# Heads of a two-layer graph network: PSUM banks in a fixed round, and conv1's constants moved ahead of the first statistics

## The chip, the cores and the metric

The kernel runs on one core of one Trainium2 chip. The metric is the device time of one execution, in microseconds. A profile is one execution recorded by the hardware profiler; its span is the time between its first and last recorded instruction, and the execution's own time is a little longer.

The engines are named as the profile names them: PE is TensorE's matmuls, PEld its weight loads, DVE is VectorE, ACT is ScalarE, POOL is GpSimd, SP is SyncE, which here only issues transfers. Lines such as L227 are lines of the kernel before the change.

## The reference

Two layers work on `x` of 128 graphs x 128 nodes x 256 channels, with an adjacency matrix per graph. Only the first steps of layer 0 matter here:

```python
h = jnp.maximum(_layernorm(x, axis=-1), 0.0)
# layer 0, on h
xc = jnp.transpose(h, (0, 2, 1))
c = relu(bn1(conv1d(xc, conv1_w, pad=0)))          # 1x1
c = bn2(conv1d(c, conv2_w, pad=8))                 # 17 taps
x_conv = transpose(relu(c + xc))
# message passing on h (distances, exp, mask, matmul), then a GRU gate
x = x + gru(concat([x_conv, x_nmp]), h)
# layer 1: graph convolutions on five groups of the first 25 nodes
```

`bn(h) = h * scale + shift` with `scale = g / sqrt(v + eps)` and `shift = b - m * scale`, per channel.

## The kernel before, in words

The graphs are worked in 32 blocks of four (`NBLK` = 32, `BB` = 4). The 17-tap convolution is done as products of spectra: 68 frequencies over a length of 136. The kernel has these stages:

1. The heads, to about 277 us. For each block: load, layer norm, transpose, conv1 with bn1 and relu, and the transform of the result into spectra. Between these steps the taps of conv2 are transformed into spectra as well, in 16 pieces of four groups each, 64 groups in all, and written to DRAM (`vd`).
2. The spectral products (`spectral`), to about 454 us, which read `vd` back as `v` and write `yd`.
3. The gates of the 32 blocks with messages, edges and layer 1 woven in, to the end.

In the heads the order on every engine is the order in which the code is written (`tc.manual_schedule()`). Behind them only GpSimd's order is by hand for a while, and the rest is ordered by Tile's scheduler. The scheduler may also place instructions of later code among the heads: it does so with the short chain on the fusion weights (L472 to L486).

The steps that the prediction names are these.

- `bank()` (L89) takes one tile of a PSUM pool with eight buffers, each a whole bank of 128 x 512 floats. A tile waits until the buffer that it gets has been read by the engine that empties it. Which of the eight buffers a tile gets is left to Tile.
- `weight_spectra` (L157) makes one piece of the taps' spectra: four groups of eight matmuls (L164) into four banks. ScalarE copies three of the banks out (L172) and VectorE the fourth (L170), except in a piece's last group, where ScalarE copies all four. When a piece is finished ScalarE issues the write of 2176 KB to `vd` (L174). `some_spectra()` (L378) runs one group per call.
- `head_stats` takes the layer norm's mean and variance of a block on VectorE (L191, L192, L195) and the power -0.5 on GpSimd (L197). `head_norm` applies them on VectorE (L203). `head_turn` transposes the block into two banks (L213), and ScalarE reads them with a relu (L214).
- `head_conv1` multiplies half a block with conv1's weights `wc1` into one bank (L227). VectorE empties it, adding bn1's shift (L230). `head_relu` follows on ScalarE (L234).
- `head_spectra` transforms a block into four banks (L243). ScalarE and VectorE empty two banks each (L253, L251).
- `heads` (L256) loops over the blocks. Iteration i runs conv1 of half of block i, a group of tap spectra, conv1 of the other half, the turn of block i + 1, a second group, and `head_spectra` of block i - 1. Statistics run three blocks ahead, normalising two. Every eighth iteration has an extra group.
- `constants` (L115) is a generator with two steps. The first, on VectorE and GpSimd, works out scale and shift of both batch norms from `vec` (L122 to L127) and spreads bn1's over a tile `bnb` (L130). The second turns `bnb` with an identity into rows on TensorE (L134), which ScalarE copies to `bnr` (L135); VectorE multiplies `wc1` by the scale (L136) and adds two gate biases (L137).

Transfers into SBUF are issued by SP, in the order taps, x, `wc1`, `fd`, further x and taps, `fw`; `gt` and `vec` are issued by ScalarE's queue at the start.

The code around the start of the heads is this:

Of the kernel before, what the change touches and what calls it, by code (L numbers as in the profile page):

```python
# [8 lines left out]
F32 = mybir.dt.float32  # L9
# [4 lines left out]
P = 128  # L14
# [53 lines left out]
V_BN1, V_BN2, V_IH, V_HH, V_B1, V_B2 = 0, 8, 16, 22, 28, 48  # L68
# [6 lines left out]
def gnn_kernel(ctx: ExitStack, tc: tile.TileContext, io, out0: bass.AP, out1: bass.AP):  # L75
# [8 lines left out]
    front = ExitStack()  # L84
    hc = front.enter_context(tc.tile_pool(name="hc", bufs=1))
    dram = ctx.enter_context(tc.tile_pool(name="dram", bufs=1, space=bass.MemoryType.DRAM))
    psum = ctx.enter_context(tc.tile_pool(name="psum", bufs=8, space=bass.MemoryType.PSUM))

    def bank():  # L89
        return psum.tile([P, 512], F32, tag="bank", name="bank")  # L90

    def row(name, n):

# [17 lines left out]
    def constant_loads():  # L111
        nc.sync.dma_start(wc1, io["wc1"].rearrange("(c p) o -> p c o", p=P))
        nc.sync.dma_start(fd, io["fd"])

    def constants():  # L115


        for j, v0 in enumerate((V_BN1, V_BN2)):
            g, b, m, v = (vec[:, v0 + 2 * q:v0 + 2 * q + 2] for q in range(4))
            sc, sh = bn[:, j, 0, :], bn[:, j, 1, :]  # L120
            ve = cst.tile([P, C], F32, name=f"bnve{j}")
            nc.vector.tensor_scalar(ve, v, EPS, None, op0=ALU.add)  # L122
            rs = cst.tile([P, C], F32, name=f"bnrs{j}")
            nc.gpsimd.tensor_tensor(rs, ve, mhalf[:, :C], op=ALU.pow)
            nc.vector.tensor_mul(sc, g, rs)
            nc.vector.tensor_mul(ve, m, sc)
            nc.vector.tensor_sub(sh, b, ve)  # L127

        bnb = hc.tile([P, 2 * C, P], F32, name="bnb")
        nc.vector.tensor_copy(bnb, bn[:, 0].rearrange("p q c -> p (q c)")[:, :, None].to_broadcast([P, 2 * C, P]))  # L130
        yield
        psb = bank()
        for q in range(2 * C):
            nc.tensor.matmul(psb[:, q * P:(q + 1) * P], bnb[:, q, :], ident, start=True, stop=True)  # L134
        nc.scalar.copy(bnr.rearrange("p q d -> p (q d)"), psb)  # L135
        nc.vector.tensor_mul(wc1, wc1, bnr[:, 0:1, :].to_broadcast([P, C, D]))  # L136
        nc.vector.tensor_add(brz, vec[:, V_IH:V_IH + 4], vec[:, V_HH:V_HH + 4])  # L137
        yield

# [9 lines left out]
    def taps_load(pool, c, q, queue, split=1, amid=None):  # L149
        w2 = pool.tile([P, WCH // 4, P], F32, tag="w2", name="w2", bufs=3)  # L150
        for t in range(0, WCH // 4, WCH // 4 // split):
            queue.dma_start(w2[:, t:t + WCH // 4 // split], io["w2t"][:, c, q, t:t + WCH // 4 // split])
            if amid:
                amid.pop()()
        return w2
# [23 lines left out]
    def head_load(pool, ahead, i, queue):  # L179
        xs[i] = pool.tile([P, BB, D], F32, tag="ln", name="ln", bufs=ahead)  # L180
        queue.dma_start(xs[i], x[i])

    def head_stats(wk, i, parts=(0, 1)):

        for h in parts:
            if not h:
                stats[i] = (wk.tile([P, BB, 2], F32, tag="mv", name="mv", bufs=3),
                            wk.tile([P, BB, 6], F32, tag="st", name="st", bufs=2))
            mv, st = stats[i]
            for b in range(h * BB // 2, (h + 1) * BB // 2):  # L190
                nc.vector.bn_stats(st[:, b, :], xs[i][:, b, :])  # L191
                nc.vector.bn_aggr(mv[:, b, :], st[:, b, :])  # L192
            if h:
                ve = wk.tile([P, BB], F32, tag="ve", name="ve", bufs=2)
                nc.vector.tensor_scalar(ve, mv[:, :, 1], EPS, None, op0=ALU.add)  # L195
                rs = wk.tile([P, BB], F32, tag="rs", name="rs", bufs=3)
                nc.gpsimd.tensor_tensor(rs, ve, mhalf, op=ALU.pow)  # L197
                stats[i] = mv, rs

    def head_norm(i):  # L200
        mv, rs = stats.pop(i)
        for b in range(BB):
            nc.vector.tensor_scalar(xs[i][:, b, :], xs[i][:, b, :], mv[:, b, 0:1], rs[:, b:b + 1],  # L203
                                    op0=ALU.subtract, op1=ALU.mult)
# [149 lines left out]
    with front as es:  # L354
        hk = es.enter_context(tc.tile_pool(name="hk", bufs=1))
        xp = es.enter_context(tc.tile_pool(name="xp", bufs=1))
        X1 = xp.tile([P, C, NP_ - NB, 2, P], F32)
        order = es.enter_context(ExitStack())
        order.enter_context(tc.manual_schedule(engines={nc.gpsimd.engine}))
        early = es.enter_context(ExitStack())  # L360
        xe = early.enter_context(tc.tile_pool(name="xe", bufs=1, side="right"))
        X0 = xe.tile([P, C, NB, 2, P], F32)
        X = X0, X1
        with ExitStack() as ws:

            ws.enter_context(tc.manual_schedule())

            xk = ws.enter_context(tc.tile_pool(name="xk", bufs=1, side="right"))
            wp = ws.enter_context(tc.tile_pool(name="wp", bufs=1))
            ahead = 4  # L370
            todo = [(c, q) for c in range(C) for q in range(D // WCH)]
            nc.scalar.dma_start(gt, io["gt"])
            nc.scalar.dma_start(vec, io["vec"])

            taps = [taps_load(wp, *todo[0], nc.sync, split=4, amid=[lambda: head_load(xk, ahead, 0, nc.sync)])]
            spectra = []

            def some_spectra(k=1):  # L378
                for _ in range(k):
                    if not spectra and todo:  # L380
                        spectra.append(weight_spectra(wp, *todo.pop(0), taps.pop(0)))
                    if spectra and next(spectra[0], STOP) is STOP:
                        spectra.pop(0)
                        if len(todo) > 2:
                            taps.append(taps_load(wp, *todo[2], nc.sync))
                        some_spectra()

            constant_loads()
            head_load(xk, ahead, 1, nc.sync)
            taps.append(taps_load(wp, *todo[1], nc.sync))  # L390
            for k in range(2, ahead):
                head_load(xk, ahead, k, nc.sync)
            nc.sync.dma_start(fw, row("fw", 5))
            taps.append(taps_load(wp, *todo[2], nc.sync))
            head_stats(hk, 0)
            some_spectra()
            head_norm(0)
            consts = constants()
            next(consts)
            some_spectra()  # L400
            some_spectra()
            head_turn(hk, 0)
            head_stats(hk, 1)
            some_spectra()
            next(consts)
            head_norm(1)
            head_stats(hk, 2)
            some_spectra()
            heads(hk, xk, ahead, X, some_spectra)
            while spectra or todo:  # L410
                some_spectra()

        bp = es.enter_context(tc.tile_pool(name="bp", bufs=1, reuse_waits="tile"))
        spectral(bp, (X0, 0), 0, NB, {})
        early.close()
        gw = ctx.enter_context(tc.tile_pool(name="gw", bufs=1, side="right", reuse_waits="tile"))
        idm = gw.tile([P, N], F32)
        wms = gw.tile([P, C, 2, MW], F32)
        bms = gw.tile([P, 2, MW], F32)
        swm = gw.tile([P, 3, MW], F32)  # L420
        wih = gw.tile([P, 2 * C, 3 * D], F32)
        whh = gw.tile([P, C, 3 * D], F32)
        sw = [gw.tile([P, 3, 3, P], F32, name=f"sw{k}") for k in range(3)]

        def gate_loads():
            nc.sync.dma_start(wms, io["wms"].rearrange("(c p) (q o) -> p c q o", p=P, q=2))
            yield
            nc.sync.dma_start(idm, io["idm"])
            nc.sync.dma_start(bms.rearrange("p q o -> p (q o)"), row("bms", 2 * MW))
            for name, w in (("whh", whh), ("wih", wih)):  # L430
                for c in range(w.shape[1]):
                    yield
                    nc.sync.dma_start(w[:, c], io[name][c * P:(c + 1) * P])

        loads, sums = gate_loads(), gate_weights()

        def gate_steps(p):
            next(loads, None)
            if p in (36, 40, 44, 52, 56, 60, 64):
                next(sums, None)  # L440

        amid = {p: lambda p=p: gate_steps(p) for p in range(NB, NP_, 4)}
        spectral(bp, (X1, NB), NB, NP_, amid)
        for _ in sums:
            pass
        order.close()
# [773 lines left out]
```

## Time and profile before

| | us |
|---|---|
| three runs | 1884.16, 1883.59, 1886.41 (median 1884.16) |
| profiled execution | 1882.45 |
| its span | 1880.5 |
| PE busy | 1858.3 (99%) |
| PEld busy | 1593.0 (85%) |
| DVE busy | 1353.7 (72%) |
| ACT busy | 743.4 (40%) |
| POOL busy | 665.3 (35%) |

Busy times are shares of the whole span, over stages that have different limits. The ends of matmuls are modelled, so that a busy PE may hold a short stall; the distance between equal instructions of two iterations tells such a stall more surely. The row "PEclk" gives the TensorE clock that was granted, as a share of full speed.

In a timeline a row is: start us, duration us, engine, line, operation, output <- input, shape, count, and in brackets the idle time before it and what ended that.

### The profile page before, as it was taken

Reading aid. Unit: us, or ns where it says so; the run is one execution under the profiler, and the core shown is the slowest. Engines: PE = TensorE matmul, PEld = TensorE weight load, DVE = VectorE, ACT = ScalarE, POOL = GpSimd, SP = SyncE. Lnnn points to the kernel's source line nnn. Section 1 sums busy time; section 2 is a strip of 40 time slices with the busy share of each in tenths; the row PEclk is TensorE's granted clock in tenths of the full one; section 3 lists DMA queues with packets and bytes.
Section 4 is the critical chain, followed back from the end, with each engine's and each line's share of the span. In section 5 each row is a group of like instructions: output and inputs, shape, how many; then the busy total and the mean of one; then the engine's idle time right before and its main releaser. Section 6 shows DMA issues by size and latency. Waiting matters only on the chain.

```text
span 1880.5 us, 31012 instructions
## 1 busy us (share of the span) xinstructions
PE 1858.3 (99%) x10854; PEld 1593.0 (85%) x10854; DVE 1353.7 (72%) x3248; ACT 743.4 (40%) x1667; POOL 665.3 (35%) x803
## 2 busy tenths in 40 slices
PE   8999999999999999999999999999999999999998
PEld 6888888888888888888788888888788888888887
DVE  7787765455878888888656778787666678788643
ACT  4665651111443334333334433433343343334334
POOL 1111125676343544454212345444312344544200
PEclk9999999999999999999999999999999999999999
DMA  8878788997532233224234322333233333222125
GB/s 295 292 309 309 283 291 280 349 314 248 165 90 73 72 83 94 76 72 121 64 103 113 122 74 72 90 79 112 61 102 94 121 94 86 72 72 67 41 88 157
DMA packets 218330, 267.95 MB, mean 142 GB/s; under 512 B 105186, under 2 KB 181815, under 8 KB 216127
## 3 DMA queue, kind: packets, MB, share of 16 engines
q1 hardware_dynamic: 206079, 195.60, 36.1%
q10 hardware_dynamic: 12096, 70.36, 9.1%
q8 instruction: 87, 1.43, 0.3%
q14 instruction: 68, 0.56, 0.1%
HBM read 169.24 MB, written 96.67 MB: 141 GB/s over the span
## 4 chain that ended last, share of the span: by engine, by line
PE 93%; DVE 2%; DMA 2%; POOL 1%; issue 0%; SPq 0%; ACT 0%; DVEq 0%; POOLq 0%; ACTq 0%
PE bank L636 44%; PE bank L318 6%; PE bank L227 5%; PE bank L964 5%; PE bank L904 5%; PE bank L522 5%; PE bank L502 3%; PE bank L243 3%; PE bank L313 3%; PE bank L587 3%; PE bank L164 2%; PE bank L499 2%; PE bank L213 1%; PE bank L883 1%; PE bank L813 1%; PE bank L572 1%
## 5 line engine op out<-in xcount | busy, mean ns | idle before, releaser
L636 PE MATMUL bank<-t,sw 128*128 128x256 f32 x1152 | 290.9, 379 | 0.0
L649 POOL TENSOR_TENSOR u<-u,m 128x256 f32<-128x256 f32 x128 | 93.4, 730 | 499.2 <-ACT m L647 424.6
L636 PEld LDWEIGHTS bank<-t,sw 128*128 128x128 f32 x1152 | 210.6, 190 | 26.6 <-issue 2.3
L636 PE MATMUL bank<-t,wih 128*128 128x256 f32 x768 | 197.2, 379 | 0.0
L636 PEld LDWEIGHTS bank<-t,wih 128*128 128x128 f32 x768 | 143.4, 190 | 19.3 <-issue 0.5
L227 PE MATMUL bank<-wc,ht 128*128 128x256 f32 x512 | 125.5, 390 | 0.3 <-DVE wc L136 0.3
L310 POOL TENSOR_TENSOR vs<-v 128x256 f32<-128x256 f32 x134 | 98.1, 756 | 72.4 <-PE bank L313 38.1
L545 ACT ACTIVATE msg<-msg 128x512 f32<-128x512 f32 x64 | 36.9, 622 | 205.5 <-DVE msg L541 205.5
L636 PE MATMUL bank<-xc,wih 128*128 128x256 f32 x384 | 114.5, 380 | 0.0
L636 PE MATMUL bank<-t,whh 128*128 128x256 f32 x384 | 114.5, 380 | 0.0
L636 PE MATMUL bank<-xn,wih 128*128 128x256 f32 x384 | 114.2, 379 | 0.0
L964 PE MATMUL bank<-w,hh 128*125 128x256 f32 (+9 forms) x480 | 113.3, 379 | 0.0
L197 POOL TENSOR_TENSOR rs<-ve,mhalf 128x4 f32<-128x4 f32 x32 | 32.6, 1020 | 223.0 <-DVE ve L195 223.0
L636 PE MATMUL bank<-ht,whh 128*128 128x256 f32 x384 | 109.9, 380 | 0.0
L904 PE MATMUL bank<-ax,w 128*128 128x500 f32 (+8 forms) x416 | 107.0, 396 | 0.9 <-DMA w<-in_w_dram 0.9
L227 PEld LDWEIGHTS bank<-wc,ht 128*128 128x128 f32 x512 | 93.6, 192 | 15.3 <-DVE wc L136 0.6
L964 PEld LDWEIGHTS bank<-w,hh 128*125 128x125 f32 (+9 forms) x480 | 84.3, 177 | 18.0 <-issue 0.9
L682 ACT ACTIVATE nn<-nn,vec 128x512 f32<-128x512 f32 x64 | 46.2, 722 | 134.1 <-DVE nn L681 134.1
L307 DVE SCALAR_TENSOR_TENSOR s<-X 128x256 f32<-128x256 f32 x67 | 46.2, 691 | 66.5 <-PE bank L318 66.5
L654 DVE TENSOR_TENSOR u<-bank,u 128x256 f32<-128x256 f32 x128 | 53.5, 418 | 54.5 <-PE bank L636 54.2
L172 ACT COPY sp<-bank 128x272 f32<-128x272 f32 x208 | 66.7, 401 | 63.0 <-PE bank L164 61.9
L502 PEld LDWEIGHTS bank<-idm,ym 128*128 128x128 f32 x512 | 66.0, 196 | 26.4 <-issue 24.0
(206 smaller groups left out, 4449.0 us busy)
## 6 DMA issues: line engine op xcount, KB each, us to landing
vd<-sp ACTq DMA_DIRECT2D x16, 2176.0 KB
v<-vd SPq DMA_DIRECT2D x34, 1024.0 KB
w<-in_w_dram SPq DMA_DIRECT2D x40, 512.0 KB
ln<-in_x_dram SPq DMA_DIRECT2D x32, 512.0 KB
htd<-ht ACTq DMA_DIRECT2D x32, 512.0 KB
yd<-ys ACTq DMA_DIRECT2D x32, 512.0 KB
ht<-htd SPq DMA_DIRECT2D x32, 512.0 KB
ym<-yd SPq DMA_DIRECT2D x32, 512.0 KB
```

Source lines behind the costliest of these rows:

```text
L172: nc.scalar.copy(dst, s)
L227: nc.tensor.matmul(pv[:, bb, :], ht[:, c, b * N:(b + 1) * N], wc1[:, c, :], start=c == 0, stop=c == C - 1)
L243: nc.tensor.matmul(ps[:, bb * LW:(bb + 1) * LW], h1[:, 2 * h + bb, c * P:(c + 1) * P], fd, start=True, stop=True)
L310: nc.gpsimd.tensor_tensor(vs[:, c], vr[c], vi[c], op=ALU.add)
L313: nc.tensor.matmul(p1[:, :D], a[:, c], vs[:, c], start=c == 0, stop=c == C - 1)
L318: nc.tensor.matmul(ps[:, k * D:(k + 1) * D], u[:, c], w[c], start=c == 0, stop=c == C - 1)
L502: nc.tensor.matmul(ps[:, b * N:(b + 1) * N], ym[:, b, o * P:(o + 1) * P], idm, start=False, stop=b == BB - 1)
L522: nc.tensor.matmul(ps[:, b, :], d[:, b * N:(b + 1) * N], w, start=True, stop=True)
L636: nc.tensor.matmul(ps, w, d, start=n == 0, stop=n == len(pairs) - 1)
L649: nc.gpsimd.tensor_tensor(got["u4"], got["u2"], got["m5"], op=ALU.add)
L904: nc.tensor.matmul(pv[:, q - q0, :], w1s[k5 + g][:, c, q * P:(q + 1) * P], xv[:, c], start=c == 0, stop=c == C - 1)
L964: nc.tensor.matmul(ps[:n1, :D], hh[:, q, at:at + n1], w2s[k5 + g][:, q, :], start=q == 0, stop=q == HID // P - 1)
```

## The change

Three things are changed.

- While the heads run, `bank()` takes the banks from eight tags with one buffer each, in a strict round: tile n goes to bank n mod 8. When the heads are done this pool is closed, and a pool of eight buffers is opened as before, with waits kept per tile (`reuse_waits="tile"`).
- `constants` has three steps instead of two. The first works out bn1 alone and `bnb`; the second makes `bnr` and multiplies `wc1`; the third works out bn2 and the gate biases.
- The calls move. The first step comes ahead of the first block's statistics, the second behind the first group of tap spectra and ahead of the first normalising, the third behind the third block's statistics. One call of `some_spectra()` ahead of `heads` is dropped, so that four are left; the group that it ran is run later, by the loop.

```diff
-    psum = ctx.enter_context(tc.tile_pool(name="psum", bufs=8, space=bass.MemoryType.PSUM))
+    turns = ExitStack()
+    banks = [turns.enter_context(tc.tile_pool(name="turns", bufs=1, space=bass.MemoryType.PSUM)), 0]
 
     def bank():
-        return psum.tile([P, 512], F32, tag="bank", name="bank")
+        pool, n = banks
+        if n is None:
+            return pool.tile([P, 512], F32, tag="bank", name="bank")
+        banks[1] = (n + 1) % 8
+        return pool.tile([P, 512], F32, tag=f"bank{n}", name="bank")
...
     def constants():
-        for j, v0 in enumerate((V_BN1, V_BN2)):
+        def scales(j, v0):
...
+        scales(0, V_BN1)
         bnb = hc.tile([P, 2 * C, P], F32, name="bnb")
...
         nc.vector.tensor_mul(wc1, wc1, bnr[:, 0:1, :].to_broadcast([P, C, D]))
+        yield
+        scales(1, V_BN2)
         nc.vector.tensor_add(brz, vec[:, V_IH:V_IH + 4], vec[:, V_HH:V_HH + 4])
         yield
...
             taps.append(taps_load(wp, *todo[2], nc.sync))
+            consts = constants()
+            next(consts)
             head_stats(hk, 0)
             some_spectra()
+            next(consts)
             head_norm(0)
-            consts = constants()
-            next(consts)
             some_spectra()
             some_spectra()
             head_turn(hk, 0)
             head_stats(hk, 1)
             some_spectra()
-            next(consts)
             head_norm(1)
             head_stats(hk, 2)
-            some_spectra()
+            next(consts)
             heads(hk, xk, ahead, X, some_spectra)
...
+        turns.close()
+        banks[:] = [ctx.enter_context(tc.tile_pool(name="psum", bufs=8, space=bass.MemoryType.PSUM, reuse_waits="tile")), None]
```

## The prediction

> **What bounds the kernel now.** I read the page first (busy shares, then the chain that ended last), then the chain in order of time for the first 600 us, then timelines of single iterations, the waits of the DMA queue, and windows for the clock.
>
> ```profile
> PE 1858.3 (99%) x10854; PEld 1593.0 (85%) x10854; DVE 1353.7 (72%) x3248; ACT 743.4 (40%) x1667; POOL 665.3 (35%) x803
> PE 93%; DVE 2%; DMA 2%; POOL 1%; issue 0%; SPq 0%; ACT 0%; DVEq 0%; POOLq 0%; ACTq 0%
> ```
>
> TensorE carries 93% of the chain, so only its stalls can be won. Its idle time is 22.2 us of 1880.5, but a stalled matmul can also read as busy, so I measure stalls by the period of a loop. In the heads (33 to 277 us) the chain shows each iteration's `head_spectra` (L243):
>
> ```profile
> 41.68 2.05 PE bank L243 x16
> ...
> 49.60 2.06 PE bank L243 x16
> ...
> 58.44 2.05 PE bank L243 x16
> ...
> 83.13 2.06 PE bank L243 x16
> ...
> 92.69 2.05 PE bank L243 x16
> ...
> 100.62 2.05 PE bank L243 x16
> ```
>
> Periods: 7.92, 8.84, then 9.56 (an iteration with an extra group of weight spectra) and 7.93. From 92.69 to 148.18 seven iterations in a row take 7.93, with DVE 45.17 and ACT 34.76 busy of 55.49 us and not one wait of PE itself; so 7.93 is TensorE's own work. The timelines of a long and a short iteration show the rest:
>
> ```profile
> 53.31 0.50 PE L164 MATMUL bank<-gt,w 17*128 17x136 f32 x4
> 53.49 0.69 DVE L230 TENSOR_TENSOR h<-bank,bnr 128x512 f32<-128x512 f32 x1
> 54.23 0.73 PE L164 MATMUL bank<-gt,w 17*128 17x136 f32 x12 [0.42 <-DVE h L230]
> 62.15 0.74 PE L164 MATMUL bank<-gt,w 17*128 17x136 f32 x16
> ```
>
> At 53.31 the group starts, then needs the bank of the conv1 that ran just ahead of it, and waits until VectorE has emptied that bank (ends 54.18). At 62.15 the same group runs through.
>
> **The change, part by part.**
>
> *Strict round.* An iteration takes 16 banks: conv1, 4, conv1, 2 of `head_turn`, 4, 4 of `head_spectra`: two whole rounds. Each tile then waits for the one eight back. Going through an iteration that starts with `head_spectra` at 0 (rows from 108.47 on): conv1 starts at 1.9 and needs the first ScalarE copy of the second group, done by 1.4; the first group, at 3.8, needs copies done by 2.4; the second, at 7.2, needs L230 from 4.6 and copies from 5.5; `head_spectra` at 7.9 needs L230 from 7.2 for its second bank. Everything is free in time, the first with 0.4 to 0.5 us to spare. Removed: seven iterations of 8.84 (ending at 41.68, 58.44, 75.21, 166.57, 183.34, 200.10 and 216.87) at 0.91 each, 6.4 us; and two of 9.56, at 92.69 and 157.74, against 8.80 for the third of that kind (225.67), 1.5 us. Sum 7.9. After an extra group the four ScalarE copies of the group before it may end 0.1 to 0.2 late; I take 0.3 off for all.
>
> *One group later.* `some_spectra()` is called four times ahead of `heads` instead of five. The 64 groups stay; one of them, 0.87 us in an iteration ((7.93 − 6.18)/2, 6.18 being the period without groups, 255.82 to 262.01), moves behind the first `head_spectra`.
>
> *conv1's constants first.* Nothing is added or removed here, but every engine's order moves:
>
> ```profile
> SPq L152 <- DMA vec<-in_vec_dram: 0.9, 1, 0.9
> ```
>
> ```profile
> 10.60 0.16 DVE L122 TENSOR_SCALAR bnve<-vec 128x2 f32<-128x2 f32 x1
> 10.84 0.70 POOL L124 TENSOR_TENSOR bnrs<-bnve,mhalf 128x2 f32<-128x2 f32 x1 [1.58 <-DVE bnve L122]
> ```
>
> `vec` lands at 5.4 (SP's issue, held back 0.9 us by it, goes out at 5.42). From L122 to the end of the copy L130 is 1.85 us, so VectorE begins the statistics at 7.3, not 5.64, and all behind them on VectorE waits. TensorE ended its first group at 4.8 and now stands at L134 until 7.4 (before it stood until 5.98 for taps). Then, at the slow rates of the first 22 us: L134 2.0 to 9.4, two groups 2.5 to 11.9, turn 2.2 to 14.1, a group to 15.4, conv1 to 19.1. Before, that conv1 ended at 21.3: TensorE is 2.2 ahead.
>
> VectorE is not. Statistics 2.4 to 9.8, copy 0.4, `wc1` product 0.7, normalising 1.4 to 12.3 (before 10.7). In the built order the six fusion-weight instructions (L472 to L486) come next, with ScalarE's L476 between: 1.5; two copies 0.8: 14.7. Statistics 2.4, GpSimd's L197 1.2, normalising 1.4: 19.7. Statistics 2.4: 22.1. Then `scales(1)`: its power on GpSimd queues behind the statistics' own L197 (1.03 + 0.7), so VectorE stands 1.8 and reaches the first L230 at 24.8. Before:
>
> ```profile
> 22.43 0.68 DVE L230 TENSOR_TENSOR h<-bank,bnr 128x512 f32<-128x512 f32 x1
> ```
>
> In the strict round the sixth group takes that bank, so TensorE, there at 22.9 (warm) or 24.1, stands until 25.5. Conv1, group, conv1, turn, group follow with two waits of 0.5 for ScalarE's turn and for L230; the first `head_spectra` runs as if from 33.2, against 32.8, with one group less done. Loss 0.4 + 0.87 = 1.3. The rows of `fw` (landed somewhere before 20.08) leave 0 to 0.8 more if it lands after 12.7; I take 0, since 3.6 MB issued ahead of it at the window's 290 to 400 GB/s are through at about 12.
>
> *Behind the heads.* The built order of all engines is the same as before, and nearly all waits; the pool is opened again with per-tile waits. The last `vd` write goes out after the second relu of iteration 28, not after the last copies of 27: old time 257.4 instead of 251.71. With 6 us gained it starts at the same absolute time, its load of `v` lands by 268.3 as before, and TensorE asks at 271: cost 0, and up to 6 if that cover is gone. The rest is paced by TensorE and moves along.
>
> Sum: 7.9 − 0.3 − 1.3 = 6.3; I take 6.0, as each of the three start-up waits costs TensorE some 0.1 to refill.
>
> **A rule against it.** The clock rows:
>
> ```profile
> 460.00:461.00 1.00, 0.00 (x0) 0.00 (x0) 1.00 (x4) 0.97 (x2) 1.00 (x2) 1.00 0.12 31
> 462.00:463.00 1.00, 1.00 (x3) 0.24 (x2) 0.38 (x1) 0.00 (x0) 0.35 (x1) 0.50 0.92 313
> 467.00:468.00 1.00, 1.00 (x6) 0.35 (x9) 0.40 (x2) 1.00 (x2) 0.18 (x1) 0.50 0.89 337
> ```
>
> An idle of 1.74 us (to 461.06) was followed by a granted clock of 0.50 for some 6.7 us. The new wait of 1.4 to 2.6 us at 22.9 to 25.5 could do the same; 6.7 at half speed is 3.3 us, and the sum falls to 2.7. The Trainium skill, "TensorE: Matmul & The Clock Gate", section "HAM oscillation — how this bites in real kernels", asks only that gaps stay under about 3.4 us; by it the sum stays 6.0. The same page's "A second HAM failure mode: psum-queue depth-cycling" says that cycling through PSUM banks made the clock oscillate; here the granted clock is 1.00 over 32.84 to 249.45, gaps of 0.42 included, so no row supports it. I keep the loss for a rival, because in the sum the gap is short when the clock is still slow at 20 us.
>
> **Rivals.**
>
> 1. *The start-up gap slows the clock.* For: the row above. Against: from 20 to 25 us the slow clock fills the gap with work. 1884.2 − 2.7 = 1881.5.
> 2. *Slower: ScalarE holds conv1.* The strict round ties conv1's first bank to the first copy after ScalarE's relu in every iteration. For: only 0.45 us of room (copy done 101.90, weight load 102.39). Against: ScalarE is 63% busy and on time in every short iteration. It decides once ScalarE is over 0.45 late; at 0.85 late it costs 0.4 × 28 = 11 us: 1889.
> 3. *The loads of `v` swallow it.* For: DMA is 0.96 busy from 249 to 277. Against: 3 us of room. It decides when the first loads land 3 us later; at 6 the time is 1884.
> 4. *The banks were not the cause*, or the round moves the waits on to L230: the stalls stay and the start costs 1.3: 1885.5. Against: the one-to-one row 53.31 to 54.23.
>
> **How the numbers follow.** The profiled execution took 1882.45 us (span 1880.5 and 1.95 around it); less 6.0 it is 1876.45. The median of the three runs is 1884.16, 1.7 above it; less 6.0 it is 1878.2, my forecast. About 0.2%, or 3.8 us, is what a measurement can tell from no change: faster is below 1880.4, slower above 1887.9. Chances: forecast 0.60 (its own range 1875.5 to 1880.4), rival 1 0.17, rival 2 0.09, rival 3 0.07, rival 4 0.07. Faster: 0.60 and 0.05 of rival 1, whose loss may be partial. Same: 0.12 of rival 1, 0.07 of rival 3, 0.01 of rival 4. Slower: 0.09 and 0.06, what rivals 2 and 4 leave with other mishaps. The range goes from 1875.0 (no start-up loss, and the runs' own scatter) to 1884.5, which takes in rivals 1 and 3.
>
> **What would show it.** Right: every iteration of the heads at 7.93, the three with an extra group at 8.8 to 9.0, no "DVE h L230" in front of L164 after 40 us, the first L302 near 271, later stages as long as before. In the start: L134 at 7.4, the first conv1 at 15.4, the first L230 near 24.8, TensorE idle before it. Wrong: periods over 8 with ScalarE's copy as releaser (rival 2), clock 0.50 at 25 to 32 (rival 1), a wait on `v` at 271 (rival 3), or 8.84 still there (rival 4).

## The result, and the profile after

| kernel | median us | runs, lowest to highest | ratio to before, 95% interval |
|---|---|---|---|
| before | 1887.26 | 1883.59 to 1889.03 | |
| after | 1886.04 | 1880.52 to 1893.52 | 1.0001 [0.9989, 1.0013] |

The forecast was 6.0 us less; the runs show no difference within about 2 us. 1886.04 lies above the range of 1875.0 to 1884.5. The median of before itself came out 3.1 us above the one that the range was worked out from (1884.16); it is the ratio that tells, and by it nothing was gained. The profiled execution took 1891.3 us (span 1889.4), among the longest of its kernel; a second profile stands below ("After, again"). Line numbers of the kernel after are 5 to 10 higher: L134 became L140, L164 became L172, L227 L235, L230 L238, L243 L251, L174 L182.

The page of the kernel after, first the busy shares, then the shares of the chain by engine:

```profile
PE 1860.9 (98%) x10854; PEld 1595.3 (84%) x10854; DVE 1353.5 (72%) x3248; ACT 744.2 (39%) x1667; POOL 665.6 (35%) x803
...
PE 91%; DMA 3%; DVE 2%; POOL 1%; SPq 1%; issue 1%; ACT 0%; ACTq 0%; DVEq 0%; POOLq 0%
```

PE is still the bound, but has 2% less of the chain. Where the stalls of before were, the chain in order of time (start us, duration us, what) now has this:

```profile
37.58 2.05 PE bank L251 x16
...
45.51 2.05 PE bank L251 x16
...
53.44 2.05 PE bank L251 x16
...
125.93 2.05 PE bank L251 x16
...
146.14 2.05 PE bank L251 x16
...
163.71 2.05 PE bank L251 x16
```

Three things are to be seen. The periods are 7.93, and no iteration of 8.84 is left in the whole stage. The first `head_spectra` starts 4.7 us later than before (37.58 against 32.84). And two iterations took 20.21 between 125.93 and 146.14 instead of 15.86, and the two behind them, with an extra group, 17.57 instead of 16.73. The timelines show both losses. First the start, on TensorE, VectorE and GpSimd:

```profile
22.05 1.04 PE L221 MATMUL bank<-ident,ln 128*128 128x128 f32 x8
...
23.02 1.01 POOL L205 TENSOR_TENSOR rs<-ve,mhalf 128x4 f32<-128x4 f32 x1 [3.83 <-DVE bnve L127]
24.00 0.70 POOL L129 TENSOR_TENSOR bnrs<-bnve,mhalf 128x2 f32<-128x2 f32 x1
...
24.73 0.16 DVE L130 TENSOR_TENSOR bn<-vec,bnrs 128x2 f32<-128x2 f32 x1 [1.72 <-POOL bnrs L129]
...
25.27 0.69 DVE L238 TENSOR_TENSOR h<-bank,bnr 128x512 f32<-128x512 f32 x1
...
26.01 1.29 PE L172 MATMUL bank<-gt,w 17*128 17x136 f32 x16 [2.93 <-DVE h L238]
```

TensorE is done with the turn at 23.1 and stands until VectorE has emptied conv1's first bank. VectorE in turn waits 1.72 for GpSimd's power of the third step, queued behind that of the statistics, as the prediction had it. Windows of the same trace (us from:to, length, busy of PE, PEld, DVE, ACT, POOL, granted clock, DMA share, GB/s) show what follows:

```profile
24.00:25.00 1.00, 0.00 (x0) 0.00 (x0) 0.24 (x2) 0.00 (x0) 0.69 (x2) 1.00 1.09 470
...
26.00:27.00 1.00, 0.99 (x16) 0.97 (x16) 0.97 (x4) 1.00 (x2) 0.00 (x0) 0.50 0.86 341
...
34.00:36.00 2.00, 2.00 (x7) 1.50 (x6) 0.02 (x1) 0.00 (x0) 0.00 (x0) 0.50 0.00 0
36.00:37.00 1.00, 1.00 (x12) 0.83 (x14) 1.00 (x3) 0.49 (x1) 0.00 (x0) 1.00 0.00 0
```

The clock is 0.50 from 26 to 36 us. The second loss, on ScalarE and TensorE:

```profile
133.90 0.33 ACTq L223 DMA_DIRECT2D htd<-ht  x1
...
134.29 3.48 ACTq L182 DMA_DIRECT2D vd<-sp  x1
...
137.88 0.97 ACT L180 COPY sp<-bank 128x272 f32<-128x272 f32 x3 [2.97 <-issue]
...
138.31 3.68 PE L235 MATMUL bank<-wc,ht 128*128 128x256 f32 x8 [2.41 <-ACT sp L180]
```

The issue of a `vd` write, 0.33 us as a rule, occupied ScalarE's queue for 3.48 us. The copies behind it came late, and conv1 waited for the bank that the first of them frees. Behind this gap the clock fell again, to 0.60 and 0.55 in windows over 138 to 142 us, and conv1 took 3.68 instead of 1.99.

So this execution adds up, against the first profile of before: the start +4.7; the stage from the first `head_spectra` to the first spectral matmul 243.7 instead of 244.2, in which the round's gain is spent on the rows above and on a group more; and +4.7 behind the heads (1608.2 instead of 1603.5). Together +8.9, the difference of the spans.

### The profile page after: what moved, and what is told of

It is laid out like the page before. It is cut to its first block, busy times and chain, and to the rows that moved or that the text cites. A ratio compares the mean times of both kernels' runs of the same rounds, so it can differ in the third digit from the quotient of the medians.

```text
span 1889.4 us, 31044 instructions
## 1 busy us (share of the span) xinstructions
PE 1860.9 (98%) x10854; PEld 1595.3 (84%) x10854; DVE 1353.5 (72%) x3248; ACT 744.2 (39%) x1667; POOL 665.6 (35%) x803
## 4 chain that ended last, share of the span: by engine, by line
PE 91%; DMA 3%; DVE 2%; POOL 1%; SPq 1%; issue 1%; ACT 0%; ACTq 0%; DVEq 0%; POOLq 0%
PE bank L646 43%; PE bank L235 6%; PE bank L974 5%; PE bank L326 5%; PE bank L914 5%; PE bank L532 5%; PE bank L251 3%; PE bank L512 3%; PE bank L597 3%; PE bank L321 3%; PE bank L172 2%; PE bank L509 2%; PE bank L893 1%; PE bank L221 1%; PE bank L823 1%; PE bank L582 1%
## 5 line engine op out<-in xcount | busy, mean ns | idle before, releaser
L235 PE MATMUL bank<-wc,ht 128*128 128x256 f32 x512 | 130.6, 401 | 2.4 <-ACT sp L180 2.4
L235 PEld LDWEIGHTS bank<-wc,ht 128*128 128x128 f32 x512 | 96.6, 198 | 19.0 <-ACT sp L180 2.6
```

The costliest lines, as they stand in the source:

```text
L235: nc.tensor.matmul(pv[:, bb, :], ht[:, c, b * N:(b + 1) * N], wc1[:, c, :], start=c == 0, stop=c == C - 1)
```

## The experiments

Theory: the round takes out its 7.9 us, and three things give it back, namely the gap at the start with the clock's fall, the slow `vd` issues that the round ties to conv1, and later stages. Rivals: the round itself gains nothing; or the losses are chance events of one profile. Every profile is cut at two points, the first `head_spectra` ("start") and the first spectral matmul ("heads" up to it, "rest" behind it). Times in us, "heads" and "rest" as differences of points rounded to 0.1:

| kernel | start | heads | rest | span | ratio of the runs |
|---|---|---|---|---|---|
| before | 32.8 | 244.2 | 1603.5 | 1880.5 | |
| before, again | 32.7 | 244.3 | 1605.0 | 1882.0 | 0.9993 [0.9985, 1.0002] |
| after | 37.5 | 243.7 | 1608.2 | 1889.4 | 1.0001 [0.9989, 1.0013] |
| after, again | 35.7 | 239.1 | 1609.7 | 1884.5 | 0.9993 [0.9978, 1.0007] |
| round only | 32.7 | 240.9 | 1610.0 | 1883.6 | 0.998 [0.997, 0.9989] |
| constants only | 36.7 | 243.7 | 1607.4 | 1887.8 | 1.0028 [1.0016, 1.0041] |
| after, fifth group back | 33.4 | 238.8 | 1607.4 | 1879.6 | 0.9983 [0.9974, 0.9991] |
| after, third step late | 32.7 | 239.2 | 1606.3 | 1878.2 | 0.997 [0.9958, 0.9981] |
| after, `vd` by SyncE | 32.9 | 238.4 | 1604.5 | 1875.8 | 0.9985 [0.9974, 0.9997] |
| after, fifth group, `vd` by SyncE | 32.6 | 237.3 | 1605.8 | 1875.7 | 0.9983 [0.9972, 0.9994] |
| after, third step late, `vd` by SyncE | 31.0 | 238.4 | 1609.5 | 1878.9 | 0.9972 [0.9962, 0.9982] |
| round and `vd` by SyncE | 32.2 | 237.3 | 1607.2 | 1876.7 | 0.9982 [0.9969, 0.9994] |
| constants and `vd` by SyncE | 34.9 | 237.2 | 1604.7 | 1876.8 | 0.998 [0.9969, 0.9991] |
| before, `vd` by SyncE | 30.9 | 236.3 | 1607.8 | 1875.0 | 0.996 [0.9947, 0.9973] |
| the same, again | 33.8 | 236.4 | 1603.9 | 1874.1 | 0.9956 [0.9943, 0.9969] |
| the same, pool reopened | 30.9 | 236.4 | 1605.7 | 1873.0 | 0.9948 [0.9935, 0.9962] |
| round, `vd` by SyncE, plain second pool | 32.0 | 237.4 | 1612.0 | 1881.4 | 0.9972 [0.996, 0.9985] |

The ratio rests on all runs, the other columns on one profiled execution each, and that one can lie anywhere among its kernel's runs: that of round only is the slowest of ten (1885.51, median 1881.48), that of after with `vd` by SyncE the fastest of eleven (1877.70, median 1883.12). Starts differ without any fault of the order, too: before with `vd` by SyncE starts at 30.9 and at 33.8 in its first two profiles, with no wait of TensorE behind 20 us in either; the granted clock first rose at 20.58 in one and at 26.27 in the other.

### The change in its two parts

**Round only.** The kernel before, with the change's `bank()` and its second pool, and with the constants and the calls of before:

```diff
-        return psum.tile([P, 512], F32, tag="bank", name="bank")
+        pool, n = banks
...
+        return pool.tile([P, 512], F32, tag=f"bank{n}", name="bank")
...
+        turns.close()
+        banks[:] = [ctx.enter_context(tc.tile_pool(name="psum", bufs=8, space=bass.MemoryType.PSUM, reuse_waits="tile")), None]
```

> The kernel before with the strict round alone: constants and the five groups ahead of the heads stay as before. Theory (the round removes 7.9 us of stalls, and the new start and the new phase of the vd writes give it back): the start is as before, first head_spectra (L251's counterpart) at 32.8 us, clock 1.00 from 33 us on, all iterations of the heads at 7.93 except three of 8.8 to 9.1; about 7 us under the median of before, ratio about 0.996. Rival (the round itself gains nothing because the stalls only move): the first head_spectra at 32.8, but periods over 8 remain and the ratio lies at 0.999 to 1.001.

Measured: 0.998 [0.997, 0.9989], some 4 us instead of 7. No iteration of 8.84 is left, but its timeline on ScalarE and TensorE (lines 5 higher than before) has the slow issue again, now in the first iteration:

```profile
33.25 3.36 ACTq L179 DMA_DIRECT2D vd<-sp  x1
...
36.70 0.97 ACT L177 COPY sp<-bank 128x272 f32<-128x272 f32 x3 [2.85 <-issue]
37.14 1.99 PE L232 MATMUL bank<-wc,ht 128*128 128x256 f32 x8 [2.28 <-ACT sp L177]
```

That iteration takes 10.48 instead of 7.93; another with an issue of 1.77 takes 8.88; and the first spectral matmul waits 0.8 for VectorE's last copy of X. Gain of the heads by the sum, with the extra groups at 8.80 as here: 7.9 - 2.55 - 0.95 - 0.8 = 3.6; measured 3.4 (244.27 less 240.84 before rounding). The rival that the round gains nothing falls. The execution is the slowest of its ten, so these two issues say what a slow one costs, not what the usual run loses by them.

**Constants only.** The kernel after, with the pool of before:

```diff
-        pool, n = banks
...
+        return psum.tile([P, 512], F32, tag="bank", name="bank")
...
-        turns.close()
-        banks[:] = [...]
```

> The kernel after with the pool of eight banks of before (no strict round, no second pool); only the order of the constants and the missing fifth group differ from before. Theory (start): TensorE idle some 2 to 3 us near 23 to 26 us, granted clock 0.50 for some 10 us behind it, first head_spectra near 36 to 37.5 instead of 32.8, the 8.84 iterations still there; 4 to 6 us over before, ratio 1.002 to 1.003. Without the round the group ahead of conv1's emptying may still run in a free bank, so the gap may be shorter: then the clock holds, first head_spectra near 33 to 34, and the ratio is about 1.000. Rival (the round gains nothing): the ratio equals that of the whole change, 1.000.

Measured: 1.0028 [1.0016, 1.0041], about 5 us slower. The first `head_spectra` comes at 36.7, and the windows give a clock of 0.50 over 30 to 32 us behind this gap on TensorE:

```profile
28.25 0.73 PE L167 MATMUL bank<-gt,w 17*128 17x136 f32 x12 [1.16 <-DVE h L233]
```

So the new start alone costs about 5 us where the sum put 1.3; the iterations of 8.84 stay, five instead of seven. The two parts measured apart, some 4 us gained and 5 lost, leave a loss of 1 to 2 us, which lies inside the interval of the whole change (-2.1 to +2.5).

### The start

**After, again.** The changed kernel unaltered (no edit).

> The changed kernel once more, unaltered, for a second profile. Theory (the loss at the start hangs on when the clock rises: if it rises near 19 us, TensorE reaches the sixth group early, stands 2.9 us and is slowed to 0.50 for 10 us; if it rises near 24 us, there is no gap): first head_spectra either near 37.5 or near 33, with the clock of 25 to 36 us at 0.50 or 1.00 to match; one or two vd issues of over 1 us on ScalarE, at other places than in the first profile. Rival (both are fixed by the order): first head_spectra at 37.5 and a slow vd issue at 134 us again.

Measured: 0.9993 [0.9978, 1.0007]. Neither extreme came: the first `head_spectra` at 35.7, the slow `vd` issue in the same place but of 1.46 (132.46), costing 0.64. TensorE's timeline of the start:

```profile
21.81 1.99 PE L235 MATMUL bank<-wc,ht 128*128 128x256 f32 x8
23.64 1.04 PE L221 MATMUL bank<-ident,ln 128*128 128x128 f32 x8
26.84 0.74 PE L172 MATMUL bank<-gt,w 17*128 17x136 f32 x16 [2.16 <-DVE h L238]
27.99 3.55 PE L235 MATMUL bank<-wc,ht 128*128 128x256 f32 x8 [0.40 <-ACT ht L222]
```

The gap is 2.16 here, and the clock is low for about 4 us (0.56 and 0.58 over 28 to 32 us) instead of 10. The loss is there in both, its size differs.

**After, fifth group back.**

```diff
             head_stats(hk, 2)
+            some_spectra()
             next(consts)
```

> The kernel after with the fifth group of weight spectra ahead of the heads put back, behind the third statistics: TensorE gets one group (0.9 to 1.3 us) into the gap at 23 to 26 us, and the vd writes fall into the same places of the iterations as before. Theory: the gap shrinks to about 1.5 to 2 us; if the clock then holds, first head_spectra near 33.5 to 34.5 and the whole at a ratio of about 0.997; if the clock still falls to 0.50, first head_spectra near 38 and the ratio about 0.999 to 1.000 (one group more done). Rival (the round gains nothing): ratio 1.000 in either case.

Measured: 0.9983 [0.9974, 0.9991]; TensorE stands 0.56 us for L238 at 26.09, the clock stays at 1.00, and the start is 33.4, one group further on than after.

**After, third step late.** VectorE is freed early instead of TensorE filled:

```diff
             head_stats(hk, 2)
-            next(consts)
             heads(hk, xk, ahead, X, some_spectra)
+            next(consts)
```

> The changed kernel with the third step of the constants (scales(1) and brz) behind the heads. VectorE reaches the first L238 about 2.4 us earlier (near 22.9 us), with as many groups of spectra as in the changed kernel. Theory (the gap of TensorE ahead of the sixth group drops the clock): the gap falls from 2.9 us or more to 0.5 or less, granted clock 1.00 over 25 to 36 us, first head_spectra near 32 to 33.5; ratio about 0.998, 2 to 3 us under the changed kernel. Rival (the loss comes from the missing group or from noise): first head_spectra 35 to 37.5 again, ratio 0.999 to 1.000.

Measured: 0.997 [0.9958, 0.9981]. VectorE reaches the first L238 at 22.63, and TensorE does not wait for it:

```profile
22.63 0.68 DVE L238 TENSOR_TENSOR h<-bank,bnr 128x512 f32<-128x512 f32 x1
...
25.96 0.75 PE L172 MATMUL bank<-gt,w 17*128 17x136 f32 x16
```

The clock rose late, at 25.34, and stayed at 1.00; the start is 32.7, with the same number of groups as after. The same start with an early clock follows below (all losses out: clock up at 19.23, gap 0.42, clock 1.00, start 31.0). The missing group is therefore not the main loss; the gap and the clock behind it are.

The mean granted clock, which every run has, shows that this holds beyond the few profiles. In the thirteen runs of after it goes with the time: the four at 0.994 took 1891.08 to 1893.52 us, the three at 0.998 1880.52 to 1884.27. The mean over all runs is 0.9977 for before (118 runs), 0.9959 and 0.9964 for after, 0.9950 for constants only, 0.9971 with the fifth group back and 0.9976 with the third step late (five runs). A clock lower by 0.0018 over 1885 us is some 3 us (an estimate from these numbers).

### The issue of vd on ScalarE

**After, `vd` by SyncE.**

```diff
-        nc.scalar.dma_start(vd[c, q], sp)
+        nc.sync.dma_start(vd[c, q], sp)
```

> The kernel after with the sixteen writes of vd issued by SyncE instead of ScalarE. Theory (a vd write whose issue takes up to 3.48 us on ScalarE holds the copies that free conv1's bank): no issue of L182 on ScalarE, the heads from the first head_spectra to the first L310 take about 238 us instead of 243.6; the time falls by as much as the slow issues cost in a usual run, 2 to 5 us, to 1881 to 1884 (ratio 0.997 to 0.999). The start keeps its clock loss (first head_spectra near 37.5). Rival (the slow issue is a chance event of the profiled run, with no part in the median): ratio 1.000 as for the whole change.

Measured: 0.9985 [0.9974, 0.9997]; it overlaps with the second interval of after. The groups of that line (duration of one, min/median/max in ns) show that from SyncE none of the sixteen issues is slow:

```profile
L182 SPq DMA_DIRECT2D vd<-sp x16: 326/327/327, 17.6 to 247.6; - x16
```

The heads take 238.4, as expected. The start was not expected: 32.9 without a throttled clock. TensorE's timeline tells why:

```profile
20.86 3.78 PE L235 MATMUL bank<-wc,ht 128*128 128x256 f32 x8
24.43 1.22 PE L221 MATMUL bank<-ident,ln 128*128 128x128 f32 x8
25.59 0.75 PE L172 MATMUL bank<-gt,w 17*128 17x136 f32 x16
```

The second conv1 still runs at the slow rate (3.78; in after it took 1.99 at 20.21). TensorE reaches the group at 25.59, when VectorE (L238 at 24.84) has just emptied the bank, and there is no gap. In the two profiles of after, with the clock up at 18.93 and 21.43, TensorE waited and lost it; here, with the clock up at 24.81, it did not wait. That is no rule: in constants only the clock rose at 25.76 and was lost all the same. Nor does this edit cure the start: among its eleven runs are two with a mean clock of 0.994 (1886.43 and 1887.22 us).

**Both edits**, fifth group and `vd` by SyncE:

> The changed kernel with both edits: fifth group ahead of the heads and vd written by SyncE. Theory (two separate losses): no throttle at the start, no period of the heads over 8 without an extra group, ratio about 0.996, 1 to 3 us under each edit alone (0.9983 and 0.9985). Rival (both edits cure the same thing, the loss at the start): ratio 0.998 as for one of them.

Measured: 0.9983 [0.9972, 0.9994]. The heads are clean in the profile (237.3), but the time is that of the fifth group alone: the expected 0.996 is missed. **Round and `vd` by SyncE**, constants as before:

> The kernel before with the strict round and vd written by SyncE, constants as before. Theory: the round's whole 7.9 us show, the 2.6 and 0.9 us stalls behind slow vd issues seen with the round alone are gone: ratio 0.996, heads from the first head_spectra to the first L310 (its counterpart) about 236.6 us against 244.2 before and 240.9 with the round alone. Rival (later stages give part back whatever the heads do): the heads shrink to 236.6 but the ratio stays at 0.998.

Measured: 0.9982 [0.9969, 0.9994], where the round alone has 0.998. The heads are 237.3, 6.9 less than before, and the ratio stays, as the rival had it. In the median the slow issues thus weigh less than the profiles of after and of round only suggest, both slow among their runs; no two versions with the round that differ in this line alone have intervals apart.

**Before, `vd` by SyncE**, meant as a control:

> The kernel before with only the writes of vd moved to SyncE. Theory (a slow issue costs only where the strict round ties conv1 to the copies behind it): ratio 1.000, the 8.84 iterations still there. Rival (slow issues on ScalarE cost before as well): ratio 0.998 to 0.999.

Measured: 0.996 [0.9947, 0.9973], better than every version with the round. Its chain, without the round:

```profile
30.93 2.05 PE bank L243 x16
...
38.86 2.05 PE bank L243 x16
...
46.78 2.05 PE bank L243 x16
```

All iterations are at 7.93, or 8.80 with an extra group; no matmul of the heads waits for anything. What changed is the order in which the pool hands out its banks. In before a group's first two matmuls ran (the row of 53.31 under "The prediction"; a matmul of the group makes two records), and the third needed the bank of the conv1 just ahead. With `vd` on SyncE the whole group runs while VectorE is still emptying conv1's bank, so none of its four banks can be that one:

```profile
34.64 0.75 PE L164 MATMUL bank<-gt,w 17*128 17x136 f32 x16
...
34.82 0.69 DVE L230 TENSOR_TENSOR h<-bank,bnr 128x512 f32<-128x512 f32 x1
```

Why Tile, which plans the banks when the kernel is built, hands them out otherwise with this line on another engine is not shown, nor is how far apart the reuses lie in the whole program. But the stalls of before did come from the banks, and one line on another engine's queue removes them.

**Before, again**, unaltered:

> The kernel before, unaltered, for a second profile. In every other profile so far the time from the first spectral matmul to the end of the span is 1604.5 to 1610 us, in the one profile of before 1603.5. Theory A (the first profile of before was a quick one): it shows about 1607 here, and the heads with their stalls of 0.9 again from 32.8 to 277: nothing is given back behind the heads. Theory B (an earlier end of the heads is given back in later stages): it shows 1603 to 1604 again. Ratio 1.000 in both.

Measured: 0.9993 [0.9985, 1.0002], rest 1605.0, between the two theories. By chance it holds the counter-check to the round: a slow issue in the same place as with the round alone.

```profile
33.24 3.59 ACTq L174 DMA_DIRECT2D vd<-sp  x1
...
34.69 1.89 PE L227 MATMUL bank<-wc,ht 128*128 128x256 f32 x8
...
37.44 0.73 PE L164 MATMUL bank<-gt,w 17*128 17x136 f32 x12 [0.42 <-DVE h L230]
```

Here conv1 (L227) runs straight on at 34.69, and the iteration takes 8.84 as in the first profile, where that issue took 0.42. Here the old order of banks made TensorE wait 0.4 for L230 but was deaf to a late ScalarE; the round is the other way round.

**Constants and `vd` by SyncE**, one pool:

> The kernel before with the constants first and four groups ahead of the heads (as in the changed kernel), its one pool of eight banks, and vd written by SyncE. Theory: with vd off ScalarE the pool's built order reuses no bank of conv1 before five other tiles, so the 8.84 iterations are gone without the strict round; what is left is the start of the constants, 2 to 5 us worse than that of the kernel with vd from SyncE alone (first head_spectra 33 to 36 us against 30.9): ratio 0.997 to 0.9985 against 0.996. Rival (constants first costs nothing once banks come free): first head_spectra near 31 and ratio 0.996.

Measured: 0.998 [0.9969, 0.9991]: 8.84 gone, gap of 1.64, clock 0.50 over 28 to 30 us, start 34.9. The new start costs 0.2% with good banks too.

**The best version again, and all losses out.** The first is the kernel before with `vd` by SyncE; the second is after with the third step late and `vd` by SyncE.

> The kernel before with vd written by SyncE, once more, as its first ratio rested on five runs. Theory (vd on ScalarE was what led the pool to hand conv1's banks out again after three tiles, so this one line does what the strict round was to do): ratio 0.996 to 0.997 again, first head_spectra 31 to 33 us, iterations at 7.93. Rival (the five runs were lucky): ratio 0.998 like the versions with the strict round.

> The changed kernel with both losses taken out: third step of the constants behind the heads, vd written by SyncE. Theory (each loss is its own): first head_spectra near 32.7, heads without any slow vd issue, 1 us under the kernel with the late third step alone (0.997), so 0.9965; no better than the kernel before with vd from SyncE (0.996), since both then run the heads at 7.93. Rival (round and constants bring something of their own): under 0.9955.

Measured: 0.9956 [0.9943, 0.9969] and 0.9972 [0.9962, 0.9982]. The one line holds and beats both kernels; round and constants add nothing to it that the runs show.

**The second pool.** Round and `vd` by SyncE took 1880.62, the one line, measured beside it, 1876.87; of these 3.8 us the heads explain 1, and about 3 had no place. The second pool, without the round, in the kernel before with `vd` by SyncE:

```diff
+        turns.close()
+        banks[:] = [ctx.enter_context(tc.tile_pool(name="psum", bufs=8, space=bass.MemoryType.PSUM, reuse_waits="tile"))]
```

> The kernel before with vd written by SyncE and its eight-buffer pool closed and opened again behind the heads, as the change does it; no round, constants as before. Theory (the second pool is where the versions with the round lose what the one line alone keeps): TensorE's first spectral matmul waits 0.8 us more, later waits behind GpSimd's t grow by about 1 us, ratio 0.998 as with the round (0.9982), against 0.996 without the second pool. Rival (the round itself costs it, or scatter): ratio 0.996.

Measured: 0.9948 [0.9935, 0.9962], the fastest of all. The 0.8 us at the first spectral matmul does not appear. And the round with `vd` by SyncE and a second pool without `reuse_waits`:

> Strict round and vd written by SyncE, constants as before, the second pool opened without waits kept per tile. Theory (the second pool costs through its banks, whatever its waits): 0.998, first spectral matmul late by 0.8 us or more. Rival (the waits kept per tile cost it): below 0.997; or, if the plain pool must wait for all of the heads, above 0.998.

Measured: 0.9972 [0.996, 0.9985], not to be told from 0.9982. So the second pool is not to blame; by elimination the round is. Of its cost about 1 us is placed in the heads (237.3 against 236.4, mostly the 0.8 at the first spectral matmul). The rest of the table shows that more lies behind the heads: "rest" is 1608.1 on average over the ten profiles with the round and 1605.4 over the seven without it, though single values scatter over 8 and 4 us. Two pieces of this can be named. TensorE's wait for GpSimd's `t` near 1320 us is 1.35 to 1.38 in each of the ten and 0.67 to 1.22 in the seven. And in three of the ten, in none of the seven, TensorE idled 2.6 to 3.1 near 350 us and the clock fell behind it; the spectral stage then took 186 to 187 us instead of 183 to 185. Three are too few to call it an effect of the round. Why the round should do either is open.

## Why the prediction was wrong, step by step

Two steps of the sum failed, each by about 4 us: the room of conv1 in the round (7.6 forecast, some 4 gained by the round alone), and the clock behind the gap at the start, put at nothing (a loss of 1.3 forecast, 5 measured for the constants alone).

- **The strict round, 7.9 - 0.3.** Right as far as it goes: no 8.84 is left in any version with it, and the iterations with an extra group take 8.80 to 9.08 (said: 8.8 to 9.0) where no slow issue falls into them. The step that failed is the one on room: "conv1 starts at 1.9 and needs the first ScalarE copy of the second group, done by 1.4", with 0.4 to 0.5 to spare. It counted ScalarE's busy instructions, and not the issue of a DMA, which stands in the same queue. It went through the iteration from 108.47 on, where the `vd` write is issued behind the copies; in others of before it stands ahead of them:

```profile
109.52 1.24 ACT L172 COPY sp<-bank 128x272 f32<-128x272 f32 x4
...
110.79 0.33 ACTq L174 DMA_DIRECT2D vd<-sp  x1
```

```profile
33.28 0.42 ACTq L174 DMA_DIRECT2D vd<-sp  x1
33.79 0.96 ACT L172 COPY sp<-bank 128x272 f32<-128x272 f32 x3
```

  The first profile also had an issue of 1.56 among its sixteen, so the warning was there. That is rival 2, once or twice in an execution, or not at all, instead of in every iteration. The issues do not explain all that is missing: without them the round still measured 0.9982, and about 3 us of that stay open (above).
- **One group later and constants first, -1.3.** The mis-sized term. The single times held: L134 at 7.56 (said 7.4), L238 at 25.27 (said 24.8), TensorE idle until 26.0 (said 25.5). The first conv1 came at 16.36 (said 15.4). `fw` landed at 13.86, not by 12.7, and VectorE stood 1.27 for it; "I take 0" was wrong. The step that failed is "I keep the loss for a rival, because in the sum the gap is short when the clock is still slow at 20 us": the sum put the first `head_spectra` at 33.2 without it, and it came at 37.5 and 35.7. From the sixth group to the first `head_spectra` it is 7.26 with a full clock (25.59 to 32.85, after with `vd` by SyncE) and 11.50 in the first profile of after (26.01 to 37.51): 4.2 us for the clock. Together with the group (0.87) the start costs 5.6 and 3.8 us in the two profiles; constants only measure 0.28%, 5 us.
- **Rival 1 had the mechanism and too small a chance.** It was held down because "from 20 to 25 us the slow clock fills the gap with work". Whether it does hangs on when the clock rises, for one thing: at 18.93 in the first profile of after, at 24.81 in that of after with `vd` by SyncE.
- **Behind the heads, 0.** Not settled. In the first profile of after TensorE waited 3.1 us for `wih` ahead of 356.6 us, but the rest runs from 1603.5 to 1612.0 over all profiles, and the first gate block (from its first L509 to the next block's) takes 19.4 in one and 23.1 us in the other profile of the same changed kernel. The means with and without the round differ by 2.7 (above); no run ties a cause to it.
- **Rival 4, "the banks were not the cause".** False: they were, as the stalls went with the order of the banks. But the cure needed no round.
- **The sum.** 7.9 - 0.3 less about 1.5 for slow issues in a mild profile (0.64) and the first spectral matmul (0.8), less 3.8 to 5.6 for the start, leaves 0.6 to 2.4 us, and the unplaced loss of the round (about 3 us) takes that. Runs: no difference. That the three start-up waits cost 0.1 each to refill, the last 0.3 of the forecast, shows in no row by itself.

The Trainium skill, "TensorE: Matmul & The Clock Gate", section "HAM oscillation — how this bites in real kernels", asks only that gaps stay under about 3.4 us. The rows here differ: in the first 30 us a clock of 0.50 followed a gap of 1.16 (constants only), of 1.64 (constants and `vd` by SyncE), of 2.16 and of 2.93, and in full flow one of 2.41; gaps of 0.42 to 0.70, and one of 2.28 in full flow (round only, ahead of 37.14), left the clock at 1.00. The measurement decides.

The length of a gap alone does not sort these rows; its place does better. In all seventeen traces the clock, once it has risen, changes only at whole multiples of 3.41 us from that first rise. Counted in such steps up to the end of the spectral products, the clock was kept where TensorE idled up to 1.82 us in one step, and fell at the end of steps with 2.06 or more; the gap of 2.28 lies across the end of a step, with 1.19 before it and 1.09 behind. The 1.16 of constants only does not fit, behind the spectral products the clock fell at less as well, and no run was made to test this reading.

## What to carry to other kernels

When a change makes TensorE reach a wait earlier, price the wait with the clock that follows it, above all in the first 30 us, where each execution's clock rises at another time (18.93 to 26.27 us in the seventeen profiles). Giving banks out in a strict order ties every tile to the engine that empties the one eight tiles back; before doing that, look what stands in that engine's queue, DMA issues included. And where a pool's bank order causes a stall, try to take the irregular work (here the `vd` writes) off the engine that frees the banks: here one line gave 0.4 to 0.5%, where the change gave nothing. That it reorders the banks for the better was luck, and has to be looked up in the profile of each kernel.

## What was not expected of the hardware

- The issue of a 2176 KB write on ScalarE's queue took 0.33 to 3.59 us in the profiles, the slow ones of over 3 us right behind the issue of a 512 KB write; the same sixteen writes issued by SyncE took 0.33 us each. The Trainium skill, "Perfetto Trace Analysis", section "DMA Instruction — HWDGE (DVE, Sync)", says that the recorded time of an issue includes a wait for the generator of descriptors; it speaks of VectorE and SyncE, which share it. Whether such a wait is what took 3 us on ScalarE here, no run shows.
- In constants only the clock fell to 0.50 behind a gap of 1.16 us, 3.41 us after it had risen. Over all profiles the stretches at 0.50 lasted 3.41, 6.83 or 10.24 us, apart from one at the very end.
